# A four-layer gated cross-attention block: attention 0's mask as a row of its keys, three batches at a time, and shared buffers

## The chip, the cores and the metric

The kernel is written for one Trainium2 chip and runs on one of its cores. A core has a matrix engine (TensorE, PE, whose weight loads are shown apart as PEld), a vector engine (VectorE, DVE), a scalar engine (ScalarE, ACT), a general engine (GpSimd, POOL) and SyncE (SP), which here only issues transfers. The metric is the time of one execution on the device, in microseconds.

## The reference, cut to what matters

x and ctx are (8, 256, 256): 8 batches of 256 tokens of 256 numbers. Four layers, each a gated cross-attention and a gated feed-forward network (FFN):

```
for l in 0..3:
    x = x + tanh(g_xattn[l]) * attention_l(layernorm(x), ctx)
    x = x + tanh(g_ffn[l])   * ffn_l(layernorm(x))
```

All attentions have 16 heads of 16 numbers. They differ in the softmax: attention 0 takes it over the keys, attention 1 over the heads, attention 2 over the keys, attention 3 over the queries. Attention 0 has a mask:

```
scores = einsum('bhqd,bhkd->bhqk', Q, K) / sqrt(16)
scores = where(mask, -inf, scores)            # mask: (1, 1, 256 queries, 256 keys)
mask   = broadcast_to(valid[0:1, None, None, :], (1, 1, 256, 256))   # the inputs': all rows alike
```

Attention 2 has a mask (8, 256) of keys by batch, all false in the inputs. FFN 0 is a mixture of 8 experts in which each expert takes its best 256 of the 2048 tokens (256 to 682 to 256). FFN 1 is one product in int8 with scales. FFN 2 is a chain of five ternary products (256 to 1024 twice, silu and gate; 1024 to 1024 with gelu, twice; 1024 to 256). FFN 3 is a mixture of 8 experts, each token to its best two, with a limit of tokens for each expert.

## The kernel before

x stays in 16 SBUF tiles of 128 tokens (`x_t`). The program runs in stages, each with its own buffers:

1. **Attention 0** for all batches, at 0–437 us. `through0(b)` is one batch: norm and transpose (`norm`, `turned`), attention (`KeyLayer.through`), then norm, transpose and router logits for FFN 0 (`rows_and_logits`). Beside it run small jobs: the NaN for a row without keys (`keyless`), the operand of FFN 1, and a check of the bits of FFN 2's weights in 44 pieces (`inexact_weights`, L1289), which tells whether they can be multiplied exactly in a faster format.
2. **FFN 0** (`ffn0`), 437–693 us: the router, then the experts, which gather tokens and scatter-add their outputs to `acc0` in DRAM. Into the router's gaps a `fill` puts the keys and values of layers 1 to 3 (`keys_and_values`), which go to DRAM (`kvd`). L926 is a matmul of one row, `emask` x the mask of layer 2, which adds the mask to a row of layer 2's keys (R_KEYMASK).
3. **`late`**, 693–1937 us: x comes back from `acc0` (L1188), the weights of layers 2 and 3 are loaded by SP (L290 to L335), and then the 8 batches go through attention 1, FFN 1, attention 2, FFN 2, attention 3 and FFN 3's router logits as a pipeline. It is written twice: a second copy for weights that aren't exact lies behind a branch (L1890) and is skipped with these inputs.
4. **FFN 3**, 1937–2279 us: router, gathers, 20 blocks of expert work, scatter-adds. The chain of work that ended last goes through its last scatter.

What orders the work: in stages 1 and 3 each batch is a Python generator that yields steps, `("P", us)` for PE, `("D", us)` for DVE, `("A", us, table)` for ACT, and takes and returns resources by `("get", name)` and `("put", name)`. `Plan` runs all generators against each other with these costs at build time and so fixes the order of the instructions of PE, DVE and ACT, each engine being in order on the chip. Lower batches go first; FFN 2's PE steps are marked "low". The resources are counts of buffers:

```
Plan(0.2, 1.0, m=4, s=2, batch0=2, layer0=2, xn_0=1, xnT_0=1, e0=2, tree=1)             # attention 0
Plan(0.5, 1.1, m=2, s=2, f=2, layer1=1, layer2=1, layer3=1, ffn1=1, ffn2=1, xn_1=1, ...,
     xnT_1=1, ..., sc=4, e2=1, e3=1, tree=1, hq=2)                                        # late
```

`m`, `s` and `f` are banks of PSUM (PE's accumulators): `f` for FFN 2, `m` for products and transposes, `s` for scores. `layerN` is the number of batches that may be inside attention N; `ffn2=1` lets one batch into FFN 2; `sc`, `e0`, `e2`, `e3` are tiles for weights of the softmax.

`KeyLayer.through` (layers 0 and 2): for each of 4 head groups, scores with the queries on the partitions for the maximum of each row (L549, maximum by DVE at L624), whose negative is then added to the queries as one more row (`shift`, L650), and scores again with the keys on the partitions (L581) for the exponentials (ACT, L635). For layer 0 each score tile begins with a 128x512 bf16 matmul of the identity by the mask times a large number: L542 with `mb` in the first pass, L574 with `mbT` in the second.

```
nc.tensor.matmul(ps[k][:, i]..., ident_b, self.mb..., start=True, stop=False)       # L542
nc.tensor.matmul(ps[k][:, i, t, :], qT[r : r + R_MAX, g, ...], kT[r : r + R_MAX, g, :], start=(l != 0), ...)   # L549
```

The sums of the weights take a detour over DRAM (`dn`, `rd`, `R`), then oT is scaled (L617), multiplied by wo (L439), and added to x (L446).

`HeadLayer` (layer 1): scores (L734), copied to SBUF by ACT (L745), then a tree of maxima over the heads, a subtraction, exponentials, a tree of sums, a reciprocal and a multiplication (L755 to L777) on DVE, and the product with the values (L790). `QueryLayer` (layer 3) goes through four rounds (two head groups by two halves of the keys): scores (L876), maxima (L846), exponentials with their sums (L852), a reciprocal (L885), the values times it (`vz`, L887), the product (L829). FFN 2: `ffn2`, products L1413, L1439, L1458, the split into a high and a low part on DVE (L1372, L1393).

Of the kernel before, what the change touches and what calls it, by code (L numbers as in the profile page):

```python
# [165 lines left out]
def flamingo_kernel(ctx: ExitStack, tc: tile.TileContext, a: dict, out: bass.AP):  # L166
# [7 lines left out]
    ps_s = ps_m = ps_o = ps_f = None  # L174
    lp = act = sm = rt = big = fw = None

    n_s = 0
# [8 lines left out]
    def psum_m(name):  # L186
        return ps_m.tile([P, 512], F32, tag="m", name=name)
# [4 lines left out]
    def open_psum(stack, n, m, o, f):  # L192
        nonlocal ps_s, ps_m, ps_o, ps_f
        ps_s = stack.enter_context(tc.tile_pool(name=f"ps_s{n}", bufs=1, space=PSUM))
        ps_m = stack.enter_context(tc.tile_pool(name=f"ps_m{n}", bufs=m, space=PSUM))
        ps_o = stack.enter_context(tc.tile_pool(name=f"ps_o{n}", bufs=o, space=PSUM)) if o else None
        if f:
            ps_f = stack.enter_context(tc.tile_pool(name=f"ps_f{n}", bufs=f, space=PSUM))
# [86 lines left out]
    def load_in(l, n, bias, pool, packed):  # L285

        if packed:
            w = pool.tile([P, 2, D], F32, tag=f"{n}{l}", name=f"{n}{l}")
            for c in range(2):
                nc.sync.dma_start(  # L290
                    out=w[:, c, :].rearrange("p (h d) -> p h d", d=DK),
                    in_=a[f"{n}{l}"][c * P : (c + 1) * P, :].rearrange("p (h r) -> p h r", r=HP)[:, :, :DK],
                )
            wb = pool.tile([P, 2], F32, tag=f"{bias}{l}", name=f"{bias}{l}")
            for g in range(NG):
                nc.sync.dma_start(
# [3 lines left out]
        else:  # L300
            w = pool.tile([P, 2, NG * P], F32, tag=f"{n}{l}", name=f"{n}{l}")
            nc.sync.dma_start(out=w, in_=a[f"{n}{l}"].rearrange("(c p) n -> p c n", p=P))
            wb = pool.tile([P, NG], F32, tag=f"{bias}{l}", name=f"{bias}{l}")
            nc.sync.dma_start(out=wb, in_=a[f"{bias}{l}"])
# [11 lines left out]
    def load_qo(l, pool, packed):  # L316
        w = load_in(l, "wq", "qb", pool, packed)
        if packed:
# [6 lines left out]
            for g in range(NG):  # L325
                nc.sync.dma_start(
# [3 lines left out]
        else:  # L330
            w["wo"] = pool.tile([P, NG, D], F32, tag=f"wo{l}", name=f"wo{l}")
            nc.sync.dma_start(out=w["wo"], in_=a[f"wo{l}"].rearrange("(c p) n -> p c n", p=P))
            if l > 0:

                nc.sync.dma_start(out=w["wo"][DK : DK + 1, 0, :], in_=a[f"ob{l}"])  # L335
# [21 lines left out]
    def norm(n, b, tag):  # L357

        yield "get", tag
# [22 lines left out]
        for t in range(2):  # L382
            o = lp.tile([P, D], F32, tag=tag, name=f"xn{n}_{b}_{t}", bufs=2)
# [5 lines left out]
        return xn  # L389

    def turn(n, b, xn, rows=None):
# [5 lines left out]
        yield "get", "m"  # L397
        yield "P", 0.6
        ps = psum_m(f"lnps{n}_{b}").rearrange("p (c t n) -> p c t n", c=2, t=2)
# [3 lines left out]
        return ps.rearrange("p c t n -> p (c t n)")  # L403

    def turned(n, b, xn, tag, rows=None):

        ps = yield from turn(n, b, xn, rows)
        yield "get", tag
        yield "A", 0.6, None
        xb = lp.tile([P, 2, S], F32, tag=tag, name=f"xnT{n}_{b}", bufs=1)  # L410
        nc.scalar.copy(xb.rearrange("p c n -> p (c n)"), ps)
        yield "put", "m"
        return xb
# [15 lines left out]
    def step_x(l, b, w, oT, ng):  # L429
        yield "get", "m"  # L430
        bias = w.get("ob")
        yield "P", 0.9 * ng + (1.2 if bias is not None else 0.0)
        po = psum_m(f"po{l}_{b}").rearrange("p (t n) -> p t n", t=2)
# [13 lines left out]
        yield "put", "m"  # L447
# [7 lines left out]
    class KeyLayer:  # L455
        def __init__(self, l, w, pool, two):
            self.l, self.w = l, w
            self.two = two
            self.V, self.nm = [], []
            for k in range(two):  # L460
# [8 lines left out]
        def through(self, b):  # L469
            l, w = self.l, self.w  # L470
            yield "get", f"layer{l}"
# [3 lines left out]
            xn = yield from norm(2 * l, b, f"xn_{l}")  # L475
            xb = yield from turned(2 * l, b, xn, f"xnT_{l}")
            yield "put", f"xn_{l}"
            qT = act.tile([P, NG, S], F32, tag=f"qT{l}", name=f"qT{l}_{b}", bufs=self.two)
            if l == 0:
                kT = act.tile([P, NG, S], F32, tag=f"kT{l}", name=f"kT{l}_{b}", bufs=self.two)  # L480
                V = self.V[b % self.two]
# [3 lines left out]
            nm = self.nm[b % self.two]  # L485

            def project(i):

                yield "get", "m"
                yield "P", 1.85  # L490
                ps = psum_m(f"qk{l}_{b}_{i}").rearrange("p (k n) -> p k n", k=2)
                if l == 0:
                    for c in range(2):
                        nc.tensor.matmul(
                            ps[:, 1, :], w["wk"][:, c, i * P : (i + 1) * P], ctxT[b][:, c, :],
                            start=(c == 0), stop=(c == 1),
                        )
                groups = (i,) if l == 0 else (2 * i, 2 * i + 1)
# [12 lines left out]
                yield "put", "m"  # L511
                yield "set", ("qk", l, b, i)

            def all_values():
                yield "get", "m"
                yield "P", 1.85
                ps = values(l, b, w, psum_m(f"v{l}_{b}"))
                yield "D", 0.7
                nc.vector.tensor_copy(V[:, :, :, 0:DK], ps.rearrange("p t (h d) -> p t h d", d=DK))
                yield "put", "m"  # L520
# [5 lines left out]
            for g in range(NG):  # L526
                if g * n_p % NG == 0:
# [3 lines left out]
                    else:  # L531
                        yield "put", f"xnT_{l}"
# [3 lines left out]
                while left:  # L536
                    ks = yield from take()
                    yield "P", 1.05 if l != 0 else 1.45 if len(ks) == 1 else 1.95
                    ps = {k: psum_s(f"mx{l}_{b}_{g}_{k}", s) for k, s in ks}
                    if l == 0:  # L540
# [5 lines left out]
                    for t in range(2):  # L546
                        for k, i in ((k, i) for k in ps for i in range(2)):
# [3 lines left out]
                                kT[r : r + R_MAX, g, :], start=(l != 0), stop=(l != 0 or t == 1),  # L551
# [5 lines left out]
            oT = act.tile([P, NG, S], F32, tag=f"oT{l}", name=f"oT{l}_{b}", bufs=self.two)  # L557
            if l == 0:
                yield "await", "mask0T"
                yield "await", ("v", l, b)  # L560
            for g in range(NG):
# [3 lines left out]
                yield "get", f"e{l}"  # L565
                e = [None, None]
                left, take = halves()
                while left:
                    ks = yield from take()
                    yield "P", 1.05 if l != 0 else 1.45 if len(ks) == 1 else 1.95  # L570
                    ps = {k: psum_s(f"sc{l}_{b}_{g}_{k}", s) for k, s in ks}
                    if l == 0:
# [5 lines left out]
                    for kt in range(2):  # L578
                        for k, i in ((k, i) for k in ps for i in range(2)):
# [3 lines left out]
                                qT[r : r + R_MAX + 1, g, :], start=(l != 0), stop=(l != 0 or kt == 1),  # L583
# [3 lines left out]
                yield "start", self.weigh(b, g, e, V, oT)  # L587
# [22 lines left out]
            yield "get", "tree"  # L610
            R = act.tile([P, NG * S], F32, tag="tree", name=f"R{l}_{b}", bufs=1)
# [6 lines left out]
            yield "put", "tree"  # L618
            yield from step_x(l, b, w, oT, NG)
            yield "put", f"layer{l}"  # L620
# [682 lines left out]
    def ffn2(b, scl, s3, exact):  # L1303
# [118 lines left out]
        if not exact:  # L1422
            yield "put", "xnT_5f"
# [549 lines left out]
```

## Time and profile before

| what | value |
|---|---|
| median of 7 runs | 2270.87 us (2254.58 to 2276.95) |
| the profiled execution | 2280.87 us, its span 2279.0 us |
| PE busy | 1884.2 us, 83% |
| PEld busy | 1368.9 us, 60% |
| DVE busy | 1196.8 us, 53% |
| ACT busy | 950.5 us, 42% |
| POOL busy | 320.1 us, 14% |
| DMA | 241.17 MB, mean 106 GB/s |

Busy times are from one execution and count neither waits nor register and branch instructions. PE's busy time is that of pipelined matmuls whose ends are modelled, and some matmul records are missing. In a group's line, `L542 PE MATMUL out<-in ... x111 | 34.3, 391 | 29.6 <-DVE nm L624 29.0` means: 111 instructions, 34.3 us busy together, 391 ns mean of one; the engine was idle 29.6 us just before them, 29.0 of it until DVE's instruction of line 624 was done. In a row of the chain of waits the numbers are the total in us, how often, and the longest.

### The profile page before, as it was taken

To read this page: it belongs to the slowest core of one execution; us is meant where nothing else is said; L and a number is where in the kernel's file an instruction comes from. 1 tells how busy PE (TensorE), PEld (TensorE's weight loads), DVE (VectorE), ACT (ScalarE), POOL (GpSimd) and SP (SyncE) were. 2 spreads that over 40 slices of the span, in tenths; PEclk is the share of its full clock that TensorE was granted. 3 is DMA by queue.
4 is the path that set the end of the run, shared out by engine and by line. 5 is a ranking of instruction groups with operands and counts; after the bars stand their busy time and mean duration, and the time that the engine had idled before them with its cause. 6 is when DMAs were issued, how large, how long until landed. Compare 5 with 4: busy or idle time off the path is not lost. (4 is left out here: it accounts for less than half of the span.)

```text
span 2279.0 us, 32300 instructions
## 1 busy us (share of the span) xinstructions
PE 1884.2 (83%) x12501; PEld 1368.9 (60%) x12540; DVE 1196.8 (53%) x2755; ACT 950.5 (42%) x1749; POOL 320.1 (14%) x378
## 2 busy tenths in 40 slices
PE   2989899699997366988898889989797884699995
PEld 1655556366464244765676667667575762588884
DVE  3654555345110787979497777979644442411110
ACT  0233223222202343756567667768566553211110
POOL 1100000000321000110111011111111210233331
PEclk7999999799998567987889889889898995799998
DMA  7221121132336001442634345443454760466662
GB/s 197 77 57 57 48 67 47 46 125 114 94 62 214 12 1 54 118 113 56 163 83 118 93 114 132 100 124 84 117 128 111 183 151 10 160 186 184 186 183 65
DMA packets 199926, 241.17 MB, mean 106 GB/s; under 512 B 36280, under 2 KB 176782, under 8 KB 197646
## 3 DMA queue, kind: packets, MB, share of 16 engines
q0 software_dynamic: 104704, 106.99, 20.7%
q1 hardware_dynamic: 87374, 124.22, 17.1%
q10 hardware_dynamic: 7680, 7.74, 1.0%
q8 instruction: 103, 1.69, 0.3%
q14 instruction: 65, 0.52, 0.1%
HBM read 203.76 MB, written 36.96 MB: 106 GB/s over the span
## 5 line engine op out<-in xcount | busy, mean ns | idle before, releaser
L635 ACT ACTIVATE e<-sc 128x1024 f32<-128x1024 f32 x128 | 128.9, 1023 | 161.2 <-PE sc L581 158.2
L624 DVE TENSOR_REDUCE nm<-mx 128x4 f32<-128x1024 f32 x128 | 153.6, 1219 | 59.9 <-PE mx L549 57.2
L1331 POOL DMA_DIRECT2D h_2T<-in_h_2T_dram x128 | 94.9, 742 | 569.2 <-PE h_2Tp L1439 464.4
L1439 PE MATMUL h_2Tp<-h,h_2T 128*128 128x256 f32 x1024 | 147.4, 301 | 13.3 <-DVE h L1372 10.8
L439 PE MATMUL po<-wo,oT 128*128 128x256 f32 x384 | 119.2, 465 | 45.0 <-DVE oT L617 37.1
L1439 PEld LDWEIGHTS h_2Tp<-h,h_2T 128*128 128x128 f32 x1024 | 134.5, 204 | 35.9 <-issue 17.8
L1439 PE MATMUL h_2Tp<-h_2T,h_2T 128*128 128x256 f32 x1024 | 143.9, 293 | 14.7 <-DVE h_2T L1372 12.8
L1439 PEld LDWEIGHTS h_2Tp<-h_2T,h_2T 128*128 128x128 f32 x1024 | 129.3, 196 | 36.2 <-issue 18.1
L1696 DVE TENSOR_SCALAR y<-d,sg 128x256 f32<-128x256 f32 x40 | 19.4, 484 | 245.7 <-PE d L1692 245.7
L1692 PE MATMUL d<-w2b,h 128*128 128x256 f32 x640 | 144.4, 379 | 0.0
L1684 ACT ACTIVATE h<-u 128x1024 f32<-128x1024 f32 x40 | 40.9, 1023 | 244.5 <-PE u L1681 244.5
L1681 PE MATMUL u<-g3T,w1b 128*128 128x256 f32 x640 | 142.7, 381 | 0.0
L1681 PEld LDWEIGHTS u<-g3T,w1b 128*128 128x128 f32 x640 | 122.4, 191 | 17.0 <-issue 0.2
L1692 PEld LDWEIGHTS d<-w2b,h 128*128 128x128 f32 x640 | 120.1, 190 | 15.5
L852 ACT ACTIVATE e<-sc,qm 128x256 f32<-128x256 f32 x256 | 117.3, 482 | 26.6 <-DVE qm L846 26.3
L385 ACT ACTIVATE xn<-x,s,y 128x256 f32<-128x256 f32 x112 | 61.2, 593 | 159.5 <-DVE s L379 148.9
L439 PEld LDWEIGHTS po<-wo,oT 128*128 128x128 f32 x384 | 85.1, 233 | 69.1 <-DVE oT L617 33.3
L1331 POOL DMA_DIRECT2D w<-in_w_2T_dram x80 | 57.5, 719 | 448.4 <-PE w L1413 270.7
L846 DVE TENSOR_REDUCE qm<-sc 128x4 f32<-128x1024 f32 x64 | 75.9, 1219 | 43.8 <-PE sc L876 43.7
L1413 PE MATMUL w<-xnT,w 128*128 128x256 f32 x512 | 81.2, 311 | 18.5 <-DVE x L1393 15.6
L758 DVE TENSOR_TENSOR hm<-hm 128x512 f32<-128x512 f32 (+2 forms) x192 | 90.1, 469 | 6.0
L1413 PEld LDWEIGHTS w<-xnT,w 128*128 128x128 f32 x512 | 71.6, 211 | 30.6 <-DVE x L1393 17.4
(349 smaller groups left out, 3738.2 us busy)
## 6 DMA issues: line engine op xcount, KB each, us to landing
h_2T<-in_h_2T_dram POOLq DMA_DIRECT2D x128, 512.0 KB, 5.2
w1b<-in_w_dram SPq DMA_DIRECT2D x20, 1024.0 KB
w2b<-in_w_dram SPq DMA_DIRECT2D x20, 1024.0 KB
w<-in_w_2T_dram POOLq DMA_DIRECT2D x64, 256.0 KB, 3.1
kvd<-kvs SPq DMA_DIRECT2D x16, 640.0 KB
kv<-kvd SPq DMA_DIRECT2D x16, 640.0 KB
R<-rd SPq DMA_DIRECT2D x64, 128.0 KB
check_h<-in_h_2T_dram SPq DMA_DIRECT2D x32, 256.0 KB
```

What stands on the lines that cost most here:

```text
L385: nc.scalar.activation(o, x_t[2 * b + t], AF.Identity, bias=shift[:, t : t + 1], scale=y[:, t : t + 1])
L439: nc.tensor.matmul(po[:, t, :], oT[:, g, t * P : (t + 1) * P], w["wo"][:, g, :], start=(g == 0 and bias is None), stop=(g == ng - 1),)
L624: nc.vector.tensor_reduce(nm[:, :, g, :].rearrange("p t (j r) -> p j t r", r=HP)[:, 2 * k : 2 * k + 2, :, R_MAX], ps, axis=AX.X, op=ALU.ma ...
L635: nc.scalar.activation(t, ps, AF.Exp, scale=0.25)
L758: nc.vector.tensor_tensor(m[:, 0:n, :], m[:, 0:n, :], m[:, n : 2 * n, :], op)
L846: nc.vector.tensor_reduce(m[:, 2 * i : 2 * i + 2], ps, axis=AX.X, op=ALU.max, negate=True)
L852: nc.scalar.activation(t[:, jj, k, :], ps[:, jj, k, :], AF.Exp, bias=m[:, j, k : k + 1], accum_out=z[:, j, k : k + 1],)
L1331: (nc.gpsimd if exact else nc.sync).dma_start(out=t, in_=src.rearrange("(c p) n -> p c n", p=P))
L1413: nc.tensor.matmul(ps[k][:, f, :], wt[k][:, c, f * P : (f + 1) * P], part[:, c, :], start=(c == 0 and i == 0), stop=(c == 1 and i == last),)
L1439: nc.tensor.matmul(ps[:, f, :], wt[c // 4][:, c % 4, f * P : (f + 1) * P], part[:, c, :], start=(c == 0 and i == 0), stop=(c == 7 and i == ...
L1681: nc.tensor.matmul(ps[:, f, :], w1[:, c, fc * P : (fc + 1) * P], gT[:, c, :], start=(c == 0), stop=(c == 1))
L1692: nc.tensor.matmul(po, h[:, fc, k * P : (k + 1) * P], w2[:, fc, :], start=(fc == 0), stop=(fc == 7))
```

## The change

- Attention 0's mask is one row, `mrow`, added to row R_KEYMASK of the keys by a matmul `emask` x `mrow` in `project`, one for each head group and batch; the matmuls of L542 and L574 and the building of `mb` and `mbT` go.
- All rows of the mask are compared with the first (`differ`), and if one differs, a second copy of attention 0 with the old matmuls is run, behind a branch that stands between attention 0 and FFN 0.
- Attention 0 takes three batches at a time instead of two, with more buffers for it.
- The bits' check has two pieces loaded ahead and a shorter planned delay.
- FFN 0's weight buffers are opened in `ffn0` and no longer before attention 0, and so are the buffers of `keys_and_values` (behind the branch).
- `late`: x is reloaded batch by batch at the head of `through` (on SP still), the loads of the weights of layers 2 and 3 are issued by ACT; FFN 2's banks and the others are one set of four; layers 1 and 3 share two places (`slot`) with their kv, qT and oT tiles; softmax weights of layers 1 to 3 share five tiles; layer 3's reciprocal and `vz` (three now) are in `weigh`, which runs beside the next round's scores; the numbers that `get` returns choose the buffer.

The core of the diff (bank numbers passed from `get` to `put` and to the tiles' tags are left out, as is the body of attention 0 that only moved into a function):

```diff
-        def __init__(self, l, w, pool, two):
+        def __init__(self, l, w, pool, places):
...
+            place = yield "get", f"layer{l}"
...
                         nc.tensor.matmul(
                             ps[:, 1, :], w["wk"][:, c, i * P : (i + 1) * P], ctxT[b][:, c, :],
-                            start=(c == 0), stop=(c == 1),
+                            start=(c == 0), stop=(c == 1 and self.mrow is None),
                         )
+                    if self.mrow is not None:
+                        nc.tensor.matmul(ps[:, 1, :], emask, self.mrow, start=False, stop=True)
...
-                    yield "P", 1.05 if l != 0 else 1.45 if len(ks) == 1 else 1.95
+                    yield "P", 1.05 if self.mb is None else 1.45 if len(ks) == 1 else 1.95
...
-                    if l == 0:
+                    if self.mb is not None:
                         for k, i in ((k, i) for k in ps for i in range(2)):
                             nc.tensor.matmul(
...
     class QueryLayer
-            for k in range(2):
+            for k in range(3):
                 v = pool.tile([P, 4, 3, DK], F32, tag=f"vz{k}", name=f"vz{l}_{k}", bufs=1)
...
-            def weigh(g, kt, e, v):
-                yield "get", "m"
+            def weigh(n, g, kt, n_e, e, m, z):
+                for i in range(2):
+                    yield "await", ("exponentials", n, i)
+                n_v = yield "get", "vz"
+                yield "D", 0.5
+                nc.vector.reciprocal(z, z)
+                v = self.vz[n_v]
+                nc.vector.tensor_tensor(
+                    v[:, :, 0:3:2, :], V[:, kt, 4 * g : 4 * g + 4, 0:3:2, :],
+                    z.unsqueeze(3).to_broadcast([P, 4, 2, DK]), ALU.mult,
+                )
+                bank = yield "get", "m"
                 yield "P", 1.05
...
-                    for i in range(2):
-                        yield "await", ("exponentials", n, i)
-                    yield "D", 0.5
-                    nc.vector.reciprocal(z, z)
-                    vz = self.vz[kt % 2]
...
-                    yield "start", weigh(g, kt, e, vz)
+                    yield "start", weigh(n, g, kt, n_e, e, m, z)
...
     def ffn0
         open_ffn(ctx, 0)
+        fw = ctx.enter_context(tc.tile_pool(name="w_ffnA", bufs=2))
...
-        for i in range(NT):
-            nc.sync.dma_start(out=x_t[i], in_=acc[i * P : (i + 1) * P, :])
...
     def inexact_weights
+        for c in range(len(pieces) + 1):
+            if c < len(pieces):
+                ahead.append(pool.tile([P, 512], F32, tag="wcheck", name=f"check_{c}", bufs=2))
+                nc.sync.dma_start(out=ahead[-1], in_=pieces[c])
+            if c > 0:
+                yield "delay", 4.0
                 yield "D", 0.7
-                nc.vector.tensor_tensor(bits, bits, t.bitcast(I32), ALU.bitwise_or)
+                nc.vector.tensor_tensor(bits, bits, ahead.pop(0).bitcast(I32), ALU.bitwise_or)
...
+                    nc.vector.tensor_tensor(
+                        m, masks["mask0"], row_all.unsqueeze(1).to_broadcast([P, 2, 256]), ALU.not_equal
                     )
...
-            plan = Plan(0.2, 1.0, m=4, s=2, batch0=2, layer0=2, xn_0=1, xnT_0=1, e0=2, tree=1)
+                plan = Plan(0.2, 1.0, m=4, s=2, batch0=3, layer0=3, xn=2, xnT=2, e=3, tree=1)
...
+        attention0(1)
+
+        with tc.If(nc.values_load(rows_differ[0:1, 0:1], min_val=0, max_val=1) > 0):
+            load_x(range(NT))
+            attention0(S)
...
     def late
-            open_psum(C, n, 2, 0, 2)
+            open_psum(C, n, 4, 0)
...
-            L2 = KeyLayer(2, load_qo(2, wp, False), wp, 1)
-            L3 = QueryLayer(3, load_qo(3, wp, True), wp)
+            L2 = KeyLayer(2, load_qo(2, wp, False, nc.scalar), wp, 1)
+            L3 = QueryLayer(3, load_qo(3, wp, True, nc.scalar), wp)
...
             def through(b):
+                for i in (2 * b, 2 * b + 1):
+                    nc.sync.dma_start(out=x_t[i], in_=acc0[i * P : (i + 1) * P, :])
                 yield from L1.through(b)
...
-                0.5, 1.1, m=2, s=2, f=2, layer1=1, layer2=1, layer3=1, ffn1=1, ffn2=1, xn_1=1, xn_2=1, xn_3=1, xn_f=1,
-                xnT_1=1, xnT_2=1, xnT_3=1, xnT_5=1, xnT_5f=1, sc=4, e2=1, e3=1, tree=1, hq=2,
+                0.5, 1.1, m=4, s=2, f=3, slot=2, layer2=1, ffn1=1, ffn2=1, ffn2_in=1, xn=2, xnT=2, e=5, tree=1, vz=3, hq=2,
```

## The prediction

> **What bounds the kernel now.** I read the strip of 40 slices first, for which engine is full in which stage.
>
> ```profile
> PE   2989899699997366988898889989797884699995
> ...
> DVE  3654555345110787979497777979644442411110
> ...
> PEclk7999999799998567987889889889898995799998
> ```
>
> A slice is 57 us. TensorE (PE) is nearly full in attention 0 (slices 2 to 7), in FFN 0's experts and in FFN 3 (the last six); in the middle it stands at 6 to 9 with VectorE (DVE) as busy. The window view puts numbers on the stages: 60–400 is attention 0 in its steady part, 440–690 FFN 0, 740–900 the head of the pipelined stage (`late`) before FFN 2's first matmuls, 900–1860 its steady part, 1860–1940 its tail, the rest FFN 3.
>
> ```profile
> core 0: us, PE busy (x) PEld busy (x) DVE busy (x) ACT busy (x) POOL busy (x), PEclk, DMA share, GB/s
> 60.00:400.00 340.00, 318.67 (x2215) 196.97 (x2250) 187.36 (x425) 104.67 (x158) 5.35 (x11) 0.99 0.19 56
> 440.00:690.00 250.00, 239.60 (x982) 145.04 (x980) 79.39 (x283) 55.81 (x112) 45.08 (x38) 0.97 0.30 93
> 740.00:900.00 160.00, 85.56 (x666) 55.19 (x659) 126.61 (x231) 51.84 (x62) 0.00 (x0) 0.63 0.06 20
> 900.00:1860.00 960.00, 831.06 (x6667) 642.30 (x6666) 685.54 (x1436) 637.31 (x1218) 148.00 (x202) 0.89 0.47 117
> 1860.00:1940.00 80.00, 40.08 (x233) 24.85 (x232) 28.34 (x87) 27.13 (x87) 2.40 (x10) 0.65 0.10 27
> ```
>
> So attention 0 is bound by PE: 319 of 340 us busy at a granted clock of 0.99, no other engine over 187. Work taken from PE there is time. In 740–900 it is DVE (127 of 160), in 900–1860 mostly PE (0.87 busy, 129 us idle), in the tail a serial chain.
>
> **Attention 0: the mask.** The groups by shape, 0–440 us:
>
> ```profile
> L542 PE MATMUL mx<-mb,ident_b 128*128 128x512 bf16 x111 | 34.3, 391 | 29.6 <-DVE nm L624 29.0
> ...
> L574 PE MATMUL sc<-mb0T,ident_b 128*128 128x512 bf16 x106 | 33.0, 382 | 0.2
> ```
>
> Each of 8 batches x 4 head groups x 4 tiles adds the mask by one matmul in the pass that finds maxima (L542) and one in the score pass (L574): 256 in all, as their 256 weight loads show (39 matmul records are missing). The recorded 217 keep PE busy 67.3 us, 0.31 each, which makes 79 us for 256; at their mean duration of 0.39 they would be 99. Pipelined neighbours overlap, so I take a value near the lower end, −84. The mask row comes back as one small matmul per head group and batch, 32. Their like is L926, which adds layer 2's mask to its keys:
>
> ```profile
> 440.00:740.00 300.00, 7.98 (x32) 2.40 (x32) 0.94 0.38 118
> ```
>
> +8 us. The score matmuls L549/L581 keep their shape and count. In the window 60–400 the 205 recorded mask matmuls keep PE busy 62.7 us, so the 240 that belong there keep it 73; relieved of these and given 7 of the new ones, PE needs 319 − 73 + 7 = 253 us there, still above DVE's 187: PE stays the bound, and three batches in flight instead of two only fill what is left of its idle time (21 of 340). I give that nothing and keep 0 to −10.
>
> Start: PE's first mask matmul waits for DVE's maxima, and DVE waits for a piece of the weight-bits check:
>
> ```profile
> 50.75 0.69 DVE L1289 TENSOR_TENSOR bits<-bits,check_w 128x512 int32<-128x512 int32 x1 [21.19 <-DMA check_w<-in_w_2T_dram]
> 52.63 1.71 PE L542 MATMUL mx<-mb,ident_b 128*128 128x512 bf16 x3 [24.91 <-DVE nm L624]
> ```
>
> That piece lands behind some 40 other loads on SP's queue, in both kernels. DVE's new order puts it ahead of the first keys' and maxima's steps, so that PE resumes a projection's step and a maximum later: 3 to 5 us, taken as +4. The new compare and reduce of the rows are about 2.4 us of DVE, hidden in its 153 idle us of that window. Attention 0: −84+8+4 = **−72**, bounds −99+8−10+3 = −98 and half of it, −36, if something else takes over.
>
> **The branch.** PE, DVE, ACT and POOL each load the flag and branch over a second copy of attention 0, in their own order, at its end. The branch behind `late` (L1890) already skips such a body:
>
> ```profile
> L1890 PEldq COMPARE_BRANCH  x1: 5286/5286/5286, 2255.8 to 2255.8; - x1
> ...
> L1890 DVEq COMPARE_BRANCH  x1: 56/56/56, 2256.3 to 2256.3; - x1
> ```
>
> PE's took 5.3 us; DVE's next instruction, a semaphore event, came at 2261.0, 4.7 us after its branch. PE's other branch (L1717) took 3.96 us. With 0.4 us for the flag's load that is 4 to 6 us at the end of a stage whose last work lies on PE and DVE; the joining path also waits for SP's and POOL's transfers, last stores that FFN 0 needs too. **+6**, range +3 to +9; a gain is excluded, since no work is taken away here. [...]
>
> **FFN 0.** Its expert weights were loaded at 48–55 us and are now asked for after the branch, with some 130 us of router and keys/values matmuls (437–570) before an expert needs them; POOL's paddings of the keys' buffers (about 2 us) move there too. Under that cover **0**; without it one weight transfer, up to +8; from a freer start −5.
>
> **Entry of `late`.** SP issued weight loads from 706.5 to 731.6 us before the first keys (kv), on which the first score matmul at 738.5 waited. Twenty-six of these loads go to ACT's queue. The first kv still stands behind all 16 reloads of x and the last store of kvd on SP, now right behind them, but the last kvd store itself waits for the fill. ACT issues its loads between its copies for that same fill, one of them waiting for the scatters: a copy queued behind that wait delays the fill. **−4**, range −12 to +8.
>
> **`late`, 740–1937.** The plan gets four common banks (before 2+2), two places shared by layers 1 and 3, five common 8-KB tiles, and layer 3's normalising moves behind its exponentials' end so that the next scores need not wait. In the built order, DVE has 168 us of its own work ahead of FFN 2's first step instead of 132, PE some 57 instead of 40: layer 1 of batches 1 and 2 is done early. FFN 2 (one batch at a time) thus starts some 25 us later, but 36 us of DVE's and 17 of PE's work are off the steady part. What PE waited for in 900–1860:
>
> ```profile
> PE av L829 <- DVE vz L887: 20.7, 8, 4.9
> PE po L439 <- DVE oT L617: 19.4, 3, 7.1
> PE w L1413 <- DVE x L1393: 15.6, 8, 6.3
> ```
>
> The first is the wait the move of `vz` aims at. I take the head start as paid back (+25 −25), 25 of the 129 idle us won (the 20.7 and a little), and the tail: layer 3 of the last batch is four rounds of about 9.5 us, one after another; overlapped, ACT's 8 x 2.8 us (four exponentials with their sums, 4 x 0.48 + 4 x 0.22) = 22 are the bound. 38 − 22 = 16 at best, −10 taken:
>
> ```profile
> L829 PE MATMUL av<-e,vz 128*32 128x256 f32 x64 | 7.7, 631 | 23.2 <-DVE vz L887 23.2
> ```
>
> **−35**, bounds −80 (PE 0.93 full, below) and +25 (head start lost, nothing else won).
>
> **Sum.** −72 + 6 + 0 − 4 − 35 = −105. The profiled execution took 2280.87 us (span 2279.0), 10 over the median of 2270.87, so 2176 there and **2166** as median.
>
> **Rivals.** (a) Head start not paid back: FFN 2's eight batches follow each other at 124 us on average in the old run (its ends go from 1007 to 1873), so a start 25 us later moves the end by 25; nothing won but the tail: `late` is +15 instead of −35, 50 more, **2216**. For it: one batch of FFN 2 at a time; against: PE's idle time there is in waits for other layers. (b) Attention 0 gives half, because DVE's maxima (1.22 us each, 128) or the hops between engines pace three batches: **2202**. Against: DVE at 0.55. (c) `late` fills PE to 0.93: 831/0.93 = 894, 66 won instead of 25: **2125**. (d) Slower: the five shared tiles. Layer 1 holds up to four of them through its DVE trees; layers 2 and 3 then find one, PE's fixed order stalls at score matmuls (L734, L876), and its share falls. The rest of the sum is −80, so it decides from 831/1040 = 0.80 down; at 0.77 it is +119 us, **2310**. For it: DVE is 0.71 busy there and 0.79 before; against: the plan orders with these tiles in its account. That the body be run instead of skipped would need a mask with differing rows; this one is one row broadcast, so I give it nothing.
>
> **How the numbers follow.** Forecast 0.50, (a) 0.20, (b) 0.10, (c) 0.12, (d) 0.08. Range 2115 to 2225: from (c) with 10 us to spare to (a) with 9; outside are (d) and the ends of (a) and (c). A measurement of this kernel tells about 0.5% (11 us) from no change: (d), with 0.01 for two of the adverse bounds at once, makes slower 0.09; the far ends of (a) and (b) give same 0.04; the rest is faster, 0.87.
>
> **What would show it.** Right: attention 0 ending at about 371 instead of 437 us with PE over 0.9 busy; 32 new matmuls of 0.25 us; a gap of 4 to 6 us on PE behind it; FFN 0 as long as before; first scores of `late` some 45 us after FFN 0's last expert; PE's share in the steady part 0.88 to 0.90 and the `vz` wait gone. Wrong: PE under 0.85 in attention 0 (b); FFN 2's eight batches as far apart as before and later (a); PE waiting at L734 or L876's new lines for tiles (d); branches far over 6 us or expert weights waited for.

## The result, and the profile after

The changed kernel takes 2289.48 us (median of 28 runs, 2261.12 to 2313.60) against 2275.01 us for the kernel before (median of 70). The ratio is 1.0018, with a 95% interval of 0.9999 to 1.0038: no change that can be told from none, where 105 us less had been forecast. The ratio counts only the fast runs of each kernel, those within 1.5% of its fastest (of the changed kernel 20 of 30, median 2276 us), and so it is smaller than 2289.48 / 2275.01. The profiled execution of the changed kernel took 2306.92 us (span 2305.1, mean granted clock 0.842), 31 us over the median of the runs that the ratio counts. So its stages below add up to 26 us more than before, which is that execution's own surplus and not the change's. Its lower clock is not: the 30 runs of the changed kernel have mean clocks of 0.841 to 0.863, 59 runs of the kernel before have 0.873 to 0.892. (The granted clock is the share of its full rate at which TensorE is allowed to run.)

The strip of the changed kernel, 40 slices of 58 us, to be laid over that of before:

```profile
PE   1999999869898738688987899898979797599996
...
DVE  2744553334410499997789678976435334411110
...
PEclk6866876679999867788898899889988995699998
```

TensorE is full in attention 0 (slices 2 to 7) as before. The clock is not: 6 to 8 tenths where it had been 9. The windows say it in numbers (60–400 is attention 0; 490–740 FFN 0; 785–950 the head of `late`; 950–1880 its steady part):

```profile
60.00:400.00 340.00, 328.97 (x1833) 208.65 (x1834) 173.38 (x368) 91.27 (x136) 8.50 (x16) 0.74 0.16 46
490.00:740.00 250.00, 236.39 (x963) 142.51 (x962) 77.21 (x273) 54.27 (x109) 48.94 (x42) 0.97 0.35 106
785.00:950.00 165.00, 94.40 (x813) 61.99 (x814) 152.44 (x251) 65.46 (x78) 0.00 (x0) 0.68 0.07 26
950.00:1880.00 930.00, 814.59 (x6415) 623.71 (x6415) 651.79 (x1392) 584.34 (x1145) 144.81 (x198) 0.89 0.49 119
```

In 60–400 TensorE is busy for 329 of 340 us, does fewer matmuls (1833 recorded, 2215 before), and has a granted clock of 0.74 instead of 0.99. The same matmuls have become longer; here the two passes of scores, first before, then after (a matmul in fp32 leaves two records here: the 256 of L549 have 512 weight loads):

```profile
L581 PE MATMUL sc<-qT,kT 18*128 18x256 f32 x488 | 64.6, 400 | 2.6
L549 PE MATMUL mx<-kT,qT 17*128 17x256 f32 x480 | 52.3, 400 | 2.7 <-DVE kT L510 1.0
```

```profile
L596 PE MATMUL sc<-qT,kT 18*128 18x256 f32 x416 | 79.7, 514 | 10.3 <-DVE nm L639 6.6 <-ACT e L649 3.5
L565 PE MATMUL mx<-kT,qT 17*128 17x256 f32 x456 | 76.8, 486 | 0.7 <-ACT e L649 0.5 <-DVE nm L639 0.3
```

Stage by stage, from the first or last instruction of each in the two profiled executions:

| stage | before, us | after, us | difference | forecast |
|---|---|---|---|---|
| attention 0, to its last router logits | 437 | 479 | +42 | −72 |
| from there to FFN 0's first transpose (the branch) | 2.5 | 8.3 | +6 | +6 |
| FFN 0, to its last scatter | 251.1 | 251.2 | 0 | 0 |
| entry of `late`, to the first scores | 48.0 | 46.4 | −2 | −4 |
| `late`, to its last router logits | 1198 | 1179 | −19 | −35 |
| FFN 3 and the end | 342 | 341 | −1 | 0 |

Most of the miss is in the first line. The records of the clock say why. In both traces it changes between 1.0 and 0.5 only, in steps of 3.4 us. From 60 us to the end of attention 0 it stands at 0.5 for 25 us before and for 228 us after. TensorE's busy time up to there is 355 us before and 401 us after. If a microsecond at 0.5 costs half of itself (the 17-row streams of experiment 8 take 0.106 us for a recorded matmul at a clock of 0.50 and 0.054 at 1.00), the same work at full clock is 343 and 287 us: an estimate of 56 us saved, and 101 us lost to the clock.

### The profile page after: what moved, and what is told of

Its sections match the earlier page's. It is cut to its first block, busy times and chain, and to the rows that moved or that the text cites. A ratio compares the mean times of both kernels' runs of the same rounds, so it can differ in the third digit from the quotient of the medians.

```text
span 2305.1 us, 31891 instructions
## 1 busy us (share of the span) xinstructions
PE 1944.7 (84%) x12317; PEld 1403.0 (61%) x12317; DVE 1198.8 (52%) x2757; ACT 927.6 (40%) x1730; POOL 321.9 (14%) x382
## 5 line engine op out<-in xcount | busy, mean ns | idle before, releaser
L1720 DVE TENSOR_SCALAR y<-d,sg 128x256 f32<-128x256 f32 x40 | 19.4, 484 | 245.7 <-PE d L1716 245.7
L565 PE MATMUL mx<-kT,qT 17*128 17x256 f32 x512 | 84.2, 489 | 29.6 <-DVE kT L526 28.8
L596 PE MATMUL sc<-qT,kT 18*128 18x256 f32 x512 | 97.7, 524 | 12.7 <-DVE nm L639 7.9
```

What stands on the lines that cost most here:

```text
L565: nc.tensor.matmul(ps[k][:, i, t, :], qT[r : r + R_MAX, g, t * P : (t + 1) * P], kT[r : r + R_MAX, g, :], start=(self.mb is None), stop=(s ...
L596: nc.tensor.matmul(ps[k][:, i, kt, :], kT[r : r + R_MAX + 1, g, kt * P : (kt + 1) * P], qT[r : r + R_MAX + 1, g, :], start=(self.mb is Non ...
```

## The experiments

**Theory 1:** the clock follows how many rows of the matmul array are in use. The mask matmuls (128 rows, 128 columns) had kept it up between the score matmuls, which use 17 or 18 of the 32 rows of each of four row groups. **Theory 2:** the order of three batches in flight gathers score matmuls into long runs, or makes TensorE stall, and that takes the clock down. In the tables, "ends" is the end of the last router logits of attention 0 in the profiled execution, the clock is that of 60–400 us unless said otherwise, and the ratio is formed as above.

**1. `rows32`: the score matmuls over 32 rows.**

```diff
-    ps[k][:, i, t, :], qT[r : r + R_MAX, g, t * P : (t + 1) * P], kT[r : r + R_MAX, g, :], ...
+    ps[k][:, i, t, :], qT[r : r + HP, g, t * P : (t + 1) * P], kT[r : r + HP, g, :], ...
-    ps[k][:, i, kt, :], kT[r : r + R_MAX + 1, g, ...], qT[r : r + R_MAX + 1, g, :], ...
+    ps[k][:, i, kt, :], kT[r : r + HP, g, ...], qT[r : r + HP, g, :], ...
```

> The changed kernel, but the score matmuls of the key layers (0 and 2) contract over all 32 rows of a head's place instead of 17 or 18; the added rows are zeros, so nothing else changes, and the number and length of the matmuls is the same. Theory 1 (the granted clock follows how many rows of the array are in use, and the removed 128-row mask matmuls had kept it up among the 17-row score matmuls): if all rows that an instruction names count, the granted clock in attention 0 rises from 0.74 to over 0.9 and the time falls to about 2190 to 2230 us; if only rows with something in them count, no change. Theory 2 (the three batches in flight put the score matmuls into longer runs, and that lets the clock fall): no change, 2289 us within 1%.

**2. `fill128` and `fill128_one`: idle matmuls in place of the mask's.**

```diff
                     ps = {k: psum_s(...) for k, s in ks}
+                    if l == 0 and self.mb is None:
+                        for k, i in ((k, i) for k in ps for i in range(2)):      # range(1) in fill128_one
+                            nc.tensor.matmul(ps[k][:, i]..., ident_b, fill_b, start=True, stop=True)
```

The same lines stand in both passes, and a 128x512 tile of ones, `fill_b`, is set up before.

> The changed kernel with 256 idle 128x512 bf16 matmuls of 128 rows in attention 0, where the mask matmuls were (their result is overwritten by the scores), the planned order unchanged. Theory 1: the granted clock in 60 to 400 us is back at 0.95 or more, attention 0 ends at about 440 us in spite of the 79 us of added work, and the time is about 2255 to 2270 us. Theory 2: the clock stays near 0.74 and the added work comes on top, 79 to 130 us: over 2360 us.

> As the run with 256 idle matmuls, but half of them (128, one for each pair of heads and pass). Theory 1: if half is enough to keep the clock up, 0.95, and 40 us less than with 256, about 2220 us; if it is not, a clock between 0.75 and 0.95 and a time between 2240 and 2290 us. Theory 2: the clock stays near 0.74, and 40 to 65 us come on top, over 2320 us.

**3. `two_batches`: the changed kernel with `batch0=2, layer0=2`.**

> The changed kernel with two batches at a time in attention 0 instead of three, all else as changed. Theory 1: the clock in attention 0 stays under 0.85, and the time within 20 us of the changed kernel's 2289 us. Theory 2: the clock is back at 0.95 or more, attention 0 ends at about 375 us, and the time is 2180 to 2210 us.

| kernel | clock | ends, us | median, us | ratio to before |
|---|---|---|---|---|
| before | 0.99 | 437 | 2275.01 | |
| changed | 0.74 | 479 | 2289.48 (2276 of the runs counted) | 1.0018 |
| rows32 | 0.88 | 419 | 2239.04 | 0.9879 (0.9833 to 0.9926) |
| fill128 | 0.88 | 490 | 2310.59 | 1.0157 (1.0092 to 1.0223) |
| fill128_one | 0.86 | 485 | 2306.61 | 1.0176 (1.0129 to 1.0222) |
| two_batches | 0.73 | 490 | 2321.13 | 1.0216 (1.0168 to 1.0264) |

Naming 14 or 15 more rows, all zeros, in matmuls of the same number and length wins 37 us over the changed kernel's 2276 and brings the clock from 0.74 to 0.88. Theory 1 had expected more: over 0.9, and 2190 to 2230 us. The window of 60–400 of `rows32`, to be read against the first line of the changed kernel's windows above (2145 recorded matmuls instead of 1833 in the same time):

```profile
60.00:400.00 340.00, 318.18 (x2145) 206.43 (x2144) 194.85 (x426) 109.67 (x163) 8.49 (x16) 0.88 0.18 55
```

The idle matmuls raised the clock to 0.88 and 0.86 too, against theory 2, which had it stay at 0.74; but theory 1 had 0.95 and 2255 to 2270 us, and the measured 2311 us is a miss, as the 2307 us with half of them are (2290 at most): with 256 of them the clock is still at 0.5 for 99 us in attention 0. Two batches didn't bring the clock back (0.73), so three batches are not what took it down. The time of that run is a miss of theory 1 too, 32 us over the changed kernel's median where 20 had been the limit. `fill128` above, `two_batches` below:

```profile
60.00:400.00 340.00, 328.19 (x1913) 193.00 (x1946) 167.28 (x357) 86.41 (x130) 8.46 (x16) 0.88 0.14 42
```

```profile
60.00:400.00 340.00, 306.42 (x1778) 194.54 (x1776) 176.85 (x400) 90.47 (x137) 8.46 (x16) 0.73 0.17 51
```

**4. `before_row`: the kernel before with the mask row alone.** The edit of `project` as in the diff of the change; no `mb` and `mbT`, no branch.

> The kernel before with the mask as a row of the keys and nothing else of the change: two batches at a time, no branch (the comparison of the mask's rows is left out, which these inputs don't need), the old late stage. Theory 1 (the 128-row mask matmuls had kept the granted clock up): the clock in 60 to 400 us falls from 0.99 to 0.70 to 0.85, attention 0 ends within 20 us of the 437 us of before, and the time is 2255 to 2290 us, although about 72 us of matmul work are gone. Rival (three batches in flight or the new buffers took the clock down): the clock stays at 0.95 or more, attention 0 ends at about 370 us and the time is about 2200 us.

**5. `masks_back` and `masks_back_two`: the changed kernel with the old mask matmuls**, three and two batches at a time.

```diff
-                    L0.mrow = wp.tile([1, S], BF16, tag="mrow0", name="mrow0")
-                    nc.vector.tensor_scalar(L0.mrow, mu, BIG, None, ALU.mult)
+                    L0.mb, L0.mbT = [wp.tile([P, 2, 256], BF16, ...) for name in masks]
+                    for o, m in zip((L0.mb, L0.mbT), masks.values()):
+                        nc.vector.tensor_scalar(o, m, BIG, None, ALU.mult)
...
```

(Left out: the masks' loads are issued ahead of those of ctx, which had gone first.)

> The changed kernel with the old mask matmuls and their planned costs in attention 0, three batches at a time, everything else as changed. Theory 1: the clock in attention 0 is back at 0.93 or more, attention 0 ends at 440 to 450 us, and the time is 2255 to 2270 us (before, plus 6 to 9 for the branch, minus the 20 us that the late stage was seen to win). Rival (three batches in flight make PE stall, and the stalls let the clock fall, mask matmuls or not): clock 0.90 or less as with the 256 idle matmuls, and a time of 2290 to 2320 us.

> As the run with the mask matmuls put back, and two batches at a time: attention 0 is then that of before, and what is left of the change is the branch, the later loads and the late stage. Theory 1 and the rival both: clock 0.96 to 0.99 in 60 to 400 us, attention 0 ends at about 437 to 442 us, and the time is 2250 to 2265 us; if it is over 2275 us, the late stage's gain of 20 us seen in the trace isn't one of the change but of that execution.

**6. `rows32_two`: 32 rows with two batches at a time; `before_row32`: the kernel before with the mask row and 32 rows.**

> The run with 32 rows in the score matmuls, with two batches at a time instead of three. If stalls of PE in the three-batch order are what drops the clock in the 32-row run (0.88 in 60 to 400 us), the clock rises over 0.93 here and the time falls to 2210 to 2225 us; if two batches leave more stalls, the clock is under 0.85 and the time 2250 to 2290 us.

> The kernel before with the mask as a row of the keys and the score matmuls of the key layers over 32 rows: two batches at a time, no branch, old late stage; the comparison of the mask's rows is left out. Theory 1 (rows in use decide the clock): the clock in 60 to 400 us is 0.85 to 0.92 instead of the 0.73 that the mask row alone gave, attention 0 ends at 405 to 425 us, and the time is 2225 to 2255 us, 50 to 80 us under the run with the row alone. Rival (the 32 rows helped only the new order or the new late stage): the clock stays under 0.8 and the time over 2280 us.

| kernel | clock | ends, us | median, us | ratio to before |
|---|---|---|---|---|
| before_row | 0.73 | 475 | 2306.07 | 1.0143 (1.0084 to 1.0203) |
| masks_back | 0.94 | 460 | 2285.26 | 1.0068 (1.0032 to 1.0104) |
| masks_back_two | 0.96 | 451 | 2282.71 | 1.0062 (1.0022 to 1.0102) |
| rows32_two | 0.90 | 425 | 2256.37 | 0.9944 (0.9908 to 0.9980) |
| before_row32 | 0.87 | 429 | 2262.38 | 0.9970 (0.9941 to 0.9998) |

The first line is the plainest: the mask row alone, in the old kernel with its two batches, takes 256 matmuls away (32 small ones come in) and makes it 1.4% slower. Theory 1 had the clock right; the loss is larger than it had (2255 to 2290 us). The window of 60–400 us of `before_row`, then of `masks_back_two`:

```profile
60.00:400.00 340.00, 309.68 (x1840) 193.22 (x1840) 164.45 (x383) 95.91 (x146) 4.10 (x8) 0.73 0.16 47
```

```profile
60.00:400.00 340.00, 319.08 (x2145) 194.48 (x2181) 188.65 (x416) 99.41 (x150) 8.47 (x16) 0.96 0.18 53
```

With the mask matmuls back the clock is back (0.94 and 0.96). The times of both `masks_back` runs missed their ranges, by 15 and 18 us. With two batches attention 0 ends at 451 us and not at 437, though its matmuls are those of before. More than these 14 us were lost at the start already: the first batch's x is updated at 136 us, before at 114, and the clock stands at 0.5 for 17 us at 86–103 us. The expectation had read a time over 2275 us as a sign that the late stage's gain isn't the change's. The trace doesn't bear that out: `late` takes 1179 us in this run too, 19 less than in the trace of before. What the rest of the change is worth, seen from the two-batch run, is then nothing: these 19 us go on the branch (+6) and this start (+14).

The 32 rows help in every combination: against the same kernel with 17 rows they win 37 us (`rows32` against the changed kernel), 44 us (`before_row32` against `before_row`) and 65 us (`rows32_two` against `two_batches`). The runs missed what was expected of them all the same: `before_row32` was to take 2225 to 2255 us, and `rows32_two`, with a clock of 0.90, lies between its two rivals (over 0.93, under 0.85) and settles nothing between them. Not all of the gain is in attention 0: the edit reaches layer 2's scores too, and in the changed kernel `late` falls from 1179 us to 1166 (`rows32`).

**7. The wait at the start.** In all these kernels TensorE stands still from about 27 to 52 us, behind a check of the weights' bits whose first piece lands late. It isn't part of the change's loss, but all the versions above have it. `rows32_check` starts the check later, in the run with 32 rows; `after_check` and `before_check` do the same in the changed kernel and in that before (there with a planned delay of 5.5 instead of 6.5).

```diff
+        yield "delay", 40.0
         for c in range(len(pieces) + 1):
...
-                yield "delay", 4.0
+                yield "delay", 3.0
```

> The changed kernel with 32 rows in the score matmuls, and the weights' bits check started 40 us later in the plan (and with a planned delay of 3 instead of 4 us for each piece), so that VectorE's first check no longer waits at 21 to 51 us for a piece behind some 40 other loads, and TensorE behind it. If that wait is all that holds TensorE there (27.7 us in the 32-row run), the time falls by 18 to 28 us, to 2210 to 2222 us; if the first batches' own inputs land as late, it falls by less than 8 us.

> The changed kernel with 17 and 18 rows in the score matmuls as it is, and the weights' bits check started later as in the run before. It tells whether the fall to 2181 us came from the 32 rows or from the later check, which also moves the order of the work. Theory 1 (the rows in use decide the clock): the clock in 60 to 360 us stays under 0.85, and only the wait of 28 us at the start is gone, so 2255 to 2270 us. Rival (the wait at the start and the order behind it had set the clock, and the rows matter little): clock 0.90 or more, 2185 to 2210 us.

> The kernel before with the bits check started later and nothing else: the wait of 25 us at the start goes, the mask matmuls stay, the clock stays at 0.97 or more in 60 to 380 us. If the wait is worth its length, 2243 to 2253 us; if the first batches wait for something else that lands as late, 2262 us or more.

| kernel | clock, 60–360 us | at 0.5 in attention 0, us | ends, us | median, us | ratio to before |
|---|---|---|---|---|---|
| before_check | 0.97 | 38 | 419 | 2252.58 | 0.9929 (0.9897 to 0.9962) |
| after_check | 0.85 | 110 | 388 | 2233.24 | 0.9850 (0.9800 to 0.9900) |
| rows32_check | 0.95 | 37 | 366 | 2180.72 | 0.9617 (0.9578 to 0.9656) |

`after_check` above, `rows32_check` below, 60–360 us; the instructions and their order are the same, only the rows differ:

```profile
60.00:360.00 300.00, 285.38 (x1958) 184.46 (x1956) 177.08 (x404) 103.79 (x153) 8.46 (x16) 0.85 0.21 63
```

```profile
60.00:360.00 300.00, 263.23 (x2003) 175.21 (x1999) 182.14 (x419) 104.85 (x155) 8.46 (x16) 0.95 0.22 66
```

In one and the same order the rows are worth 52 us. (In the profiled executions, which are 41 us apart, attention 0 has 22 us of it and `late` 16.) But the later check was worth 43 us in the changed kernel and 58 us in `rows32`, more than the wait of 28 us that it took away, and it raised the clock of 60–360 us from 0.75 to 0.85 with 17 rows: there theory 1, with its 2255 to 2270 us, was wrong, and its rival, with 0.90 and 2185 to 2210 us, was wrong too. `rows32_check` is 29 us under its own range for the same reason. So something else decides too how often the clock falls. It may be the order of the work, or that TensorE comes out of the start with a full clock (in `after_check` it is at 1.0 from 26 to 74 us); no run separates these. `rows32_check` beats both kernels: 3.8% under the kernel before.

**8. `forms` and `forms2`: the forms of matmul by themselves**, streams of fp32 matmuls with nothing else; none of the reference's work is done.

```
rows17:  for j in range(4): matmul(ps[j][:, 0:256], padded[32j : 32j+17, 0:128], padded[32j : 32j+17, :])
rows32:  the same over 32 rows, 15 of them zeros
cols32:  for j in range(4): matmul(ps[0][32j : 32j+32, 0:256], full[:, 32j : 32j+32], full)
rows128: matmul(ps[i % 4][:, 0:256], full[:, 0:128], full)
```

> A kernel by itself, with none of the reference's work (its output is a copy of x): streams of fp32 matmuls of one form each, nothing between them, each stream once after 10 to 20 us in which TensorE stands still (cold) and once right after 100 matmuls of 128 rows (warm). Forms, all with 256 columns moving: 17 rows in four row groups (as the score matmuls), 32 rows in four row groups with 15 of them zeros (as in the 32-row runs), 128 rows with 32 columns of weights in four column groups (as the products with the values), 128 rows with 128 columns. Theory 1 (rows in use decide): the 17-row stream stays at 0.5 from cold and falls to 0.5 within about 10 us from warm; the 32-row, 32-column and 128-row streams rise to 1.0 within 10 us and hold it. Rival (not the rows but stalls and the mix of the kernel decide): all four streams rise to 1.0 and hold it, since TensorE is busy throughout.

> As the kernel of streams by themselves (its output is a copy of x), mended: TensorE now really stands still for over 15 us before each cold stream, since VectorE's work in between waits for the stream before. The run before showed that a 17-row stream never rises from cold (128 us at half clock, TensorE full) but holds a full clock that it is given (65 us). Cold streams here: 17 rows, 32 rows, 32 columns, 128 rows. Then, from warm, each form in bursts of about 2.6 us with a round trip to VectorE (1 to 1.5 us) between them, 20 bursts each. Theory 1 in its new form (a stall lets the clock fall whatever the form; only enough rows in use raise it again): 32-row, 32-column and 128-row streams rise within 10 us from cold and the 17-row stream not; in bursts, the 17-row form ends at half clock and stays there, the others fall at times and come back. Rival (a stall of this length lets no form fall, so what takes the clock in attention 0 is something else): all four hold 1.0 in bursts.

In `forms` only the 17-row stream had a real pause before it (16.3 us). It ran 128 us from cold without a change, 0.107 us for each recorded matmul, and right after 128-row matmuls it ran at 0.054 us for the whole 65 us, against the theory's fall within 10 us. The two stretches, cold and warm (no clock was recorded before 150 us, so the 1.00 of the first line says nothing: 1132 matmuls take 120 us there, 1120 take 60 us in the second):

```profile
20.00:140.00 120.00, 120.00 (x1132) 99.30 (x1128) 8.62 (x8) 0.00 (x0) 1.00 0.01 1
195.00:255.00 60.00, 60.00 (x1120) 56.99 (x1116) 0.00 (x0) 0.00 (x0) 1.00 0.01 2
```

So by itself the stream got no faster in 128 us, and it held the full clock that it was given for the 65 us that it ran without a pause. The windows of `forms2`: from cold 17 rows, 32 rows, 32 columns; then, from warm, in bursts with short stalls, 17 rows, 32 rows, 32 columns (columns: busy time of TensorE, its weight loads, VectorE and POOL, then the clock):

```profile
40.00:125.00 85.00, 85.00 (x800) 69.17 (x800) 0.00 (x0) 0.00 (x0) 0.50 0.00 1
172.00:218.00 46.00, 45.59 (x800) 40.72 (x800) 0.32 (x3) 0.00 (x0) 0.94 0.01 2
263.00:308.00 45.00, 44.88 (x801) 24.58 (x802) 0.13 (x2) 0.00 (x0) 0.97 0.01 2
502.00:732.00 230.00, 200.98 (x1820) 156.47 (x1824) 23.06 (x72) 0.00 (x0) 0.50 0.00 1
762.00:902.00 140.00, 109.27 (x1921) 96.54 (x1921) 24.41 (x77) 0.00 (x0) 1.00 0.01 2
929.00:1067.00 138.00, 107.59 (x1920) 60.35 (x1920) 24.44 (x77) 0.00 (x0) 1.00 0.01 2
```

From cold, 800 recorded matmuls of 17 rows take 85 us at half clock with TensorE busy all the time; 800 of 32 rows are at full clock after about 5 us (0.94 over the window) and take 46 us. In bursts, with about 1.6 us of stall between two of them, the 17-row form is at half clock 7 us after the first stall and stays there for the other 230 us, while it is busy 87% of the time; the other two forms, busy 78%, don't fall at all in the 140 and 138 us. Theory 1's new form had them fall and come back: they do better than that.

Attention 0 of the changed kernel agrees in part. The clock fell there eleven times between 60 and 470 us. Six falls came at stalls: in the 3.4 us up to 284 us, for one, TensorE was busy 67% of the time. In the 3.4 us before the other five it was busy for 96% or more, mostly or in part with matmuls of 17 or 18 rows. So in the mix the clock is lost without a stall too, which the stream by itself didn't show. It came back, all twelve times, only after 3.4 us in which at least 2.9 us were matmuls over 128 rows. Before, the falls up to 400 us lasted 3.4 us each (146–150 us, 344–348 us); after, up to 48 us (329–377 us).

The traces of all 14 kernels say the same of the rise. In attention 0, from 60 us on and cut into the clock's steps of 3.4 us, there are 336 steps at half clock in which TensorE was busy for 95% or more. Where no matmul of 17 or 18 rows ran in them, 88 of 132 were followed by a full clock; where these took a quarter of the step or more, 3 of 165. In the traces of before and after alone it is 9 of 9 and 0 of 41.

So how busy TensorE is doesn't settle the clock by itself: the 17-row stream was busy for 85 of 85 us and stayed at 0.50, and five of the eleven falls in attention 0 came after 3.4 us in which it was busy for 96% or more.

## Why the prediction was wrong

- **The failed step** is in attention 0: "PE stays the bound" came true by the busy time (329 of 340 us after), "relieved of these and given 7 of the new ones, PE needs 319 − 73 + 7 = 253 us there" was not. It took the durations of the old trace, measured at a clock of 0.99, for work in which the matmuls that held that clock are missing. −72 was forecast, +42 measured. At full clock the work did shrink, by the estimate of 56 us above. That the kernel with 32 rows and a later check ends attention 0 at 366 us, near the 371 that the prediction named, is no support for it: the later check took the wait at the start away, which the prediction had left in, and with that wait `rows32` ends at 419. (The 371 counts the branch; 437 − 72 is 365.)
- **What I could have seen.** The window view showed 0.99 in attention 0 and 0.63 in 740–900. The prediction quotes the first and never asks what it rests on. None of the rivals has the clock in it; the slower one that I worked out (shared tiles in `late`) didn't come.
- **The start**, +4: TensorE's maxima go on at 56.3 us instead of 52.6, as forecast, but 5 us less work was done by 60 us (13.1 against 18.1 us busy), which the term left out.
- **The branch**, +6, measured +6. TensorE's branch took 3.7 us, and the router's chain waits for VectorE, whose next step comes 2.9 us after its branch:

```profile
L1883 PEldq COMPARE_BRANCH  x1: 3671/3671/3671, 477.7 to 477.7; - x1
L1883 DVEq COMPARE_BRANCH  x1: 72/72/72, 479.7 to 479.7; - x1
```

- **FFN 0** 0 and 0, as forecast. The **entry** −4 and −2 agree by luck of this pair: with the old entry, `before_row`, `before_row32` and `before_check` take 42, 42 and 43 us, and the other kernels with the new one 46 to 52. So a gain isn't shown, and a loss of 3 to 9 us is as well possible.
- **`late`**, −35, measured −19 (and −26 between `before_check` and `after_check`, 1204 and 1178 us). The mechanism was right, its size was off. FFN 2's first end comes 310 us after the first scores instead of 268, +42 where the head start was put at +25; its other seven batches take 815 us instead of 866, −51 against the −50 of the terms paid back and won; the tail after its last end is 54 us instead of 64, −10 as forecast. Even the −19 is not firm: the old late stage takes 1186 us in `before_row` and `before_row32`, which differ from the kernel before in attention 0 only. The waits in the steady part show where part of the gain went: the wait for `vz` fell from 20.7 to 11.5 us, and that for the scaled oT rose from 19.4 to 39.3 us.

```profile
PE po L454 <- DVE oT L632: 39.3, 7, 8.3
PE av L850 <- DVE vz L841: 11.5, 4, 6.3
```

- **Left open:** how mixed work moves the clock. In `rows32` it stayed at 0.5 for 27 us (109–136 us) in a stretch of which 32-row scores were 57%, a form that rose after about 5 us by itself; and 256 idle matmuls of 128 rows left 99 us at half clock. Which property of the mask matmuls held the clock wasn't tried apart either (rows, columns, type), nor any number of rows between 18 and 32, nor what the separate edits of `late` are worth.

## What to carry to other kernels

A duration from a trace holds for the clock of that trace (a score matmul of 400 ns at 0.99 took 486 to 514 at 0.74): before taking matmuls away, look which of them use all 128 rows, and whether those that stay can hold the clock by themselves (with 256 of them gone it went from 0.99 to 0.73 in `before_row`). Where a contraction in a kernel that TensorE bounds uses part of a 32-row group, try naming all 32 rows over zeros; a matmul took 0.054 us at full clock either way, and it was worth 37 to 65 us here. Where TensorE is full and its recorded matmuls get longer, read the granted clock before looking for a wait.

## What the runs showed of the hardware

- A stream of 17-row fp32 matmuls in four row groups that started after a pause kept TensorE busy at a clock of 0.50 for the 85 us that it ran (`forms2`, 0.106 us for a recorded matmul), and at 0.107 us for a recorded matmul for 128 us in `forms`; the same stream over 32 rows, 15 of them zeros, was at full clock after about 5 us (`forms2`, 0.94 over 46 us). The 15 rows held zeros, so the number of rows that the instruction names made this difference, not what is in them.
- The 17-row form by itself held a full clock for the 65 us that it ran without stalls (`forms`, 0.054 us for a recorded matmul). In bursts it lost it within 7 us of the first of its stalls (about 1.6 us each) and was at 0.50 for the 230 us that followed (`forms2`).
- In the attention, 3.4 us at half clock that were full and had a quarter or more of 17- or 18-row matmuls in them were followed by a full clock in 3 of 165 cases (0 of 41 in the traces of before and after); full ones without them, in 88 of 132 (9 of 9).
- Taking 256 matmuls of 0.31 us off a stage that TensorE bounds made it 38 us longer (437 to 475 us, `before_row`), at a clock of 0.73 instead of 0.99.
